# Due times of the rank work and the number of slot buffers in a one-core graph layer

## The chip, the cores and the metric

The kernel runs on one core of one Trainium2 chip. A core has five engines that run at the same time, each through its own list of instructions in a fixed order: PE (TensorE, the matrix unit), DVE (VectorE), ACT (ScalarE), POOL (GpSimd) and SP (SyncE, which here only issues transfers). Transfers between the chip's memory and the core's own memory are carried by DMA engines beside them. An instruction that needs another engine's result, or a transfer's data, waits on a semaphore, and everything behind it on its engine waits with it.

The metric is the device time of one execution in microseconds (us). The kernel before took 540.39 us, the median of three runs (539.81, 540.39 and 543.72).

## The reference

The layer is a graph convolution over 6250 nodes of 128 features and 100000 edges, which are sorted by destination:

```python
Xs = X[src]
m_data = Xs @ W_data.T + b_data
m_ctrl = Xs @ W_control.T + b_control
msg = jnp.where((edge_types == 0)[:, None], m_data, m_ctrl)
agg = jax.ops.segment_sum(msg, dst, num_segments=X.shape[0])
out = agg + (X @ W_self.T + b_self)
x = _layernorm(x + jax.nn.relu(out), axis=-1)
```

Each edge takes its source node's row, multiplied by one of two weight matrices by the edge's type; a destination sums its edges' rows, adds its own row times a third matrix, and the result is rectified, added to the input and normalized.

## The kernel before

The kernel gathers no row by address for most edges. It multiplies all nodes by both matrices once (`m3`: 98 blocks of 128 rows, each value kept as three bf16 parts of 128 columns, so 384 columns) and then gathers and sums with matrix products of 0/1 matrices.

**Ranges and groups.** The destinations are cut into 39 ranges of 160 nodes, numbered here from 0; a few nodes at the end are handled by a gather on POOL. The ranges form eleven groups of 1, 2 and then nine times 4 (`GROUPS`), numbered by an index from 0: index 4 holds ranges 11 to 14, index 5 (the sixth group) ranges 15 to 18, and index 10 ranges 35 to 38.

**Rank work** (`ranks`) prepares a group. For each edge of a range it finds in which of the 98 blocks the source lies and the edge's rank among the edges of that block. It loads the edges (`win`, L468), builds 0/1 matrices `hots` on DVE (L799, L803), counts on PE (L810), sends the counts to memory and back (`past`, L830 and L833), forms ranks on PE (`rk`, L846) that DVE reduces to slots (`slot`, L851), and scatters the source numbers on PE into `vt` (L890). DVE turns `vt` into `vs` (L905 to L911), and SP writes it to memory (`packed`, L917). PE multiplies once more into `vt` for the edges that found no slot (L993).

**A range's main work** (`sums`). SP copies the range's packed slots from memory to all 128 partitions (`rows<-packed`, L1043, 784 KB). DVE compares them in place with the partition number (L1053), which gives the 0/1 matrix of sources. In 25 steps PE multiplies it by `m3` (stage 1, L1075: four matmuls into one bank, `g` or `x`), ACT or DVE copies the bank to `gs` (L484, L485), and PE multiplies by the 0/1 matrix of destinations, `hot2` (built on DVE, L1061), into the sum `a` (stage 2, L1092 and L1095). After a range DVE adds the three parts (`s`, L624); after a group the rows are normalized, also with a product into `vt` (L615), and written.

**What sets the order.** Nothing in the code is in the order in which it runs. Each step is added to a plan with its engine, an estimated duration, a due number and what it reads and writes; `Plan.run` is a list scheduler that gives each engine the ready step with the lowest due number and writes all instructions in that order. The order on the chip is then fixed. Range number r has the due number `T0 + r * TW` with `T0` 36 and `TW` 13. The rank work of a group is due from `when` on:

```python
when = max(when + late + 22 * step + GAP, T0 + w0 * TW - LEAD)
```

Here `w0` is the group's first range and `LEAD` is 80, so from index 3 on rank work starts 80 units ahead of its range, and the groups are 52 units apart.

**Buffers.** A buffer ring gives a new tile the buffer of the tile that came so many before it, and the first writer of the new tile waits for all users of the old one. The packed slots have the ring `rows` with three buffers: the copy for range r can start when stage 1 of range r-3 is over. At the start of the kernel the same three buffers hold the first three of four pieces of the transposed input (`xts`), from which `m3` is made. `vt` and `rk` are one bank each, `hot2` has two buffers.

## Time and profile before

| | us |
|---|---|
| median of three runs | 540.39 |
| lowest and highest | 539.81 and 543.72 |
| the profiled execution | 542.22 |
| its span, first to last instruction | 540.4 |
| PE busy in the span | 502.1 |
| DVE busy | 441.1 |
| ACT busy | 429.0 |
| POOL busy | 201.5 |

A profile is one execution, recorded by the hardware. Its rows give the start and duration of each instruction, and by the semaphores what ended a wait. PEclk is the granted clock of PE as a share of full speed. Engine names with a q (SPq) are the engine's queue, which issues transfers and waits. A matmul's end is modelled, so that a PE that is shown as busy may still be waiting for a moment. The rows that carry the argument stand in the prediction.

### The profile page before, as it was taken

The page shows a single profiled execution, that of the slowest core. Times are in us where ns is not written, and L with a number is a line of the kernel's source. Part 1 is how long each engine was busy: PE and PEld are TensorE (multiplying, and loading weights), DVE is VectorE, ACT ScalarE, POOL GpSimd, SP SyncE. Part 2 cuts the span into 40 slices and gives each one's busy share as a digit, 9 for nine tenths or more (in the row PEclk, how much of TensorE's full clock was granted, in tenths as well). Part 3 has the DMA queues.
Part 4 walks back from the last instruction along what each step waited for, and adds up shares of the span by engine and source line. Part 5 has one row for each costly group of instructions (what it writes and reads, how often), then busy time and mean ns, then how long its engine had stood idle before and what let it go on. Part 6 is the DMA issues. An engine that isn't in the chain of part 4 may idle for free. (4 is left out here: it accounts for less than half of the span.)

```text
span 540.4 us, 30907 instructions
## 1 busy us (share of the span) xinstructions
PE 502.1 (93%) x13288; PEld 432.6 (80%) x13288; DVE 441.1 (82%) x1168; ACT 429.0 (79%) x1077; POOL 201.5 (37%) x284
## 2 busy tenths in 40 slices
PE   7799879799999988999999999999999999999991
PEld 4465557699889877888988887888898899888990
DVE  6388989889989997898989889979978678956642
ACT  4566767698889877888988878978898898878990
POOL 1000535700830684176067247707701720542000
PEclk9989899999999998999999999999999999999997
DMA  7466661540453055325413533351342352234200
GB/s 244 160 256 224 240 181 29 167 161 6 134 145 88 12 139 151 98 77 152 141 38 111 141 95 95 91 180 41 115 128 88 115 163 89 63 107 126 70 19 17
DMA packets 44932, 63.43 MB, mean 117 GB/s; under 512 B 19178, under 2 KB 35279, under 8 KB 44751
## 3 DMA queue, kind: packets, MB, share of 16 engines
q1 hardware_dynamic: 41745, 56.22, 33.5%
q0 software_dynamic: 1120, 2.23, 2.0%
q10 hardware_dynamic: 1922, 2.91, 1.7%
q8 instruction: 106, 1.74, 1.3%
q14 instruction: 39, 0.32, 0.2%
HBM read 45.61 MB, written 13.82 MB: 110 GB/s over the span
## 5 line engine op out<-in xcount | busy, mean ns | idle before, releaser
L1092 PE MATMUL a<-gs,hot 128*32 128x384 bf16 x3744 | 376.1, 328 | 0.4 <-issue 0.3
L484 ACT CAST gs<-g 128x384 bf16<-128x384 f32 x700 | 302.9, 492 | 64.3 <-PE g L1075 53.6
L1075 PE MATMUL g<-m,rows 128*32 128x384 bf16 x2958 | 327.1, 336 | 9.0 <-DVE rows L1053 5.7
L1075 PEld LDWEIGHTS <-rows 128*32 128x32 bf16 x3822 | 253.4, 134 | 27.7 <-DVE rows L1053 6.5
L1095 PE MATMUL a<-gs,hot 128*32 128x128 bf16 x2808 | 273.1, 220 | 2.1 <-issue 2.1
L1092 PEld LDWEIGHTS <-hot 128*32 128x32 bf16 x3900 | 206.4, 98 | 6.7 <-issue 3.1
L1095 PEld LDWEIGHTS <-hot 128*32 128x32 bf16 x2925 | 155.6, 97 | 14.1 <-issue 2.4
L1075 PE MATMUL x<-m,rows 128*32 128x384 bf16 x864 | 122.0, 335 | 0.0
L484 ACT CAST gs<-x 128x384 bf16<-128x384 f32 x199 | 98.3, 494 | 8.6 <-PE x L1075 5.7
L1061 DVE TENSOR_TENSOR hot<-iota_b,to_d 128x1920 bf16<-128x1920 bf16 (+2 forms) x85 | 93.1, 1105 | 0.1
L851 DVE TENSOR_REDUCE slot<-rk 124x8 f32<-124x400 f32 (+2 forms) x99 | 56.1, 567 | 22.3 <-PE g L1075 10.3
L674 POOL TENSOR_SCALAR xr<-xr,mv,rstd 128x128 f32<-128x128 f32 (+1 forms) x44 | 56.5, 1289 | 21.9 <-DVE rstd L651 18.4
L846 PE MATMUL rk<-hots,tri 128*32 128x400 bf16 (+1 forms) x388 | 51.3, 337 | 4.5 <-DVE slot L851 1.5
L1053 DVE TENSOR_SCALAR rows<-rows,pid 128x3136 bf16<-128x3136 bf16 (+1 forms) x46 | 41.6, 904 | 5.7 <-DMA rows<-packed 5.7
L937 POOL TENSOR_SCALAR pv<-slot 124x88 f32<-124x88 bf16 x9 | 9.5, 1058 | 79.6 <-DVE slot L868 74.2
L624 DVE TENSOR_REDUCE s<-a 128x128 f32<-128x384 f32 (+1 forms) x40 | 22.1, 551 | 15.7 <-ACT bs L484 9.9
L1016 POOL DMA_INDIRECT sr<-table,at x20 | 29.8, 1489 | 10.8 <-DVE at L1004 6.2
L491 POOL COPY to_d<-vs 32x100 bf16<-32x100 bf16 (+1 forms) x72 | 29.2, 406 | 5.9 <-DVE vs L911 2.7
L846 PEld LDWEIGHTS <-tri 128*32 128x32 bf16 x428 | 22.9, 96 | 9.9 <-issue 8.6
L803 DVE TENSOR_TENSOR hots<-hots,val 124x1200 bf16<-124x1200 bf16 (+3 forms) x42 | 28.0, 675 | 0.0
L799 DVE TENSOR_TENSOR hots<-iota_b,st 124x1200 bf16<-124x1200 bf16 (+3 forms) x42 | 27.6, 671 | 0.0
L767 POOL TENSOR_SCALAR pay<-u 124x88 f32<-124x88 f32 x9 | 8.9, 994 | 46.2 <-DVE u L752 45.1
(224 smaller groups left out, 667.9 us busy)
## 6 DMA issues: line engine op xcount, KB each, us to landing
rows<-packed SPq DMA_DIRECT2D x36, 784.0 KB
table<-m SPq DMA_DIRECT2D x12, 768.0 KB
xc<-in_xt SPq DMA_DIRECT2D x9, 320.0 KB
rows<-packed ACTq DMA_DIRECT2D x3, 784.0 KB
rows<-in_xt SPq DMA_DIRECT2D x8, 256.0 KB
xr<-in_x SPq DMA_DIRECT2D x8, 256.0 KB
out<-xr SPq DMA_DIRECT2D x8, 256.0 KB
gl<-sr SPq DMA_DIRECT2D x39, 48.0 KB
```

The lines of the kernel that those rows point to most:

```text
L484: [("ACT", act(cols), lambda: A.copy(o(), src())), ("DVE", dve(cols), lambda: V.tensor_copy(o(), src()))], None, None, due, r, w, lat)
L491: "POOL", 0.25 + cols * 0.0014, lambda: G.tensor_copy(o(), src()), due, r, w)
L674: fp = lambda k=k, m=m: G.tensor_scalar(h.t[:m, k, :], h.t[:m, k, :], mv.t[:m, k, 0:1], rstd.t[:m, k : k + 1], op0=ALU.subtract, op1=ALU.mult)
L803: vec(when + 2 + pace * k0, m * NC, lambda k0=k0, k1=k1, hs4=hs4, hp=hp: V.tensor_tensor(hp(), hp(), fl(val)[:, k0 * nw : k1 * nw, None, : ...
L846: T.matmul(acc.t[R * j : R * j + R, : (k1 - k0) * wide], tri.t[:, R * j : R * j + R], flat(k0, k1, P), start=True, stop=True, skip_group_c ...
L851: vec(due, (k1 - k0) * wide, lambda k0=k0, k1=k1, acc=acc: V.tensor_reduce(slot.t[:, k0:k1, :], acc.t[:EP, : (k1 - k0) * wide].rearrange(" ...
L1016: add("POOL", GC, lambda pr=pr, sr=sr: G.indirect_dma_start(out=sr.t[: room(pr)], out_offset=None, in_=table[:, :], in_offset=bass.Indirec ...
L1053: add("DVE", dve(half * NT, 0.305) + 0.05, lambda sp=sp, rs=rs: V.tensor_scalar(sp.t[:, rs], sp.t[:, rs], pid1.t, None, op0=ALU.is_equal), ...
L1061: lambda i=i, hot2=hot2, s4=s4, c0=c0, c1=c1: V.tensor_tensor(hot2.t[:, c0:c1].rearrange("p g (c d) -> p g c d", d=2), iota1_b.t.rearrange ...
L1075: T.matmul(gp.t[R * t : R * t + R, :D3], sp.t[:, :, 4 * g + t], m3.t[:, 4 * g + t, :], start=True, stop=True)
L1092: T.matmul(a.t[R * j : R * j + R, :D3], hot2.t[:, g, R * j : R * j + R], gs.t, start=g == 0, stop=False, skip_group_check=True)
L1095: T.matmul(a.t[R * c : R * c + R, D3:], hot2.t[:, g, P:], gs.t[:, c * D : (c + 1) * D], start=False, stop=last, skip_group_check=True)
```

## The change

The due number of a group's rank work is lowered by 4 for index 5, by 8 for index 6, and so on to 24 for index 10; from index 4 on the groups are so 48 apart, not 52. The ring of packed slots has two buffers. The third piece of the transposed input, which had its third buffer, gets a tile of its own.

```diff
     for j, n in enumerate(XB):
-        ring = ("rows", 3, R * NT) if j < 3 else ("hot2", 2, NS * WN)
-        xts.append(B(work, [D, 2 * n * P], BF16, *ring))
+        if j == 2:
+            xts.append(C([D, 2 * n * P], BF16, "x2"))
+        else:
+            ring = ("rows", 2, R * NT) if j < 2 else ("hot2", 2, NS * WN)
+            xts.append(B(work, [D, 2 * n * P], BF16, *ring))
...
-            sp = B(work, [P, R, NT], BF16, "rows", 3, R * NT)
+            sp = B(work, [P, R, NT], BF16, "rows", 2, R * NT)
...
-            when = max(when + late + 22 * step + GAP, T0 + w0 * TW - LEAD)
+            when = max(when + late + 22 * step + GAP, T0 + w0 * TW - LEAD - 4 * max(gi - 4, 0))
```

No instruction of the computation is added or taken away. The scheduler writes a new order, with line numbers three higher behind the first edit. Three places show what moves.

The first is SP's list where the packed slots of index 4 are written and the copies for ranges 11 and 12 follow. `past` and `hots` belong to index 5, `win` loads the edges of index 6. Before:

```order
L917 DMA packed<-vs 128x2x98
L462 TENSOR_LOAD first
L468 ISA
L468 DMA win<-in_edges 124x66
L830 DMA past<-csb 64x2x200
L462 TENSOR_LOAD first
L468 ISA
L468 DMA win<-in_edges 124x66
L1043 DMA rows<-packed 128x3136 x2
L833 DMA hots<-past 4x4400
```

Now, from `past` of the same group on:

```order
L833 DMA past<-csb 64x2x200
L462 TENSOR_LOAD first
L468 ISA
L468 DMA win<-in_edges 124x66
L836 DMA hots<-past 4x4400
L920 DMA packed<-vs 128x2x98
L1046 DMA rows<-packed 128x3136
```

The copy for range 11 stood behind two loads and `past`, and now follows the write of the slots directly; that write itself now stands behind `past` and `hots`, and the copy for range 12 comes later.

The second is DVE's list around the compare of range 11 (`rows<-rows,pid`). Before, `hot_6187` is the destination matrix of range 11, `hot_6280` that of range 12, and `s<-a` the end of range 10:

```order
L1061 TENSOR_TENSOR hot_6187<-iota_b,to_d 128x2080
L1061 TENSOR_TENSOR hot_6187<-iota_b,to_d 128x1920
L803 TENSOR_TENSOR hots<-hots,val 124x1200
L624 TENSOR_REDUCE s<-a 128x128
L1061 TENSOR_TENSOR hot_6280<-iota_b,to_d 128x2080
L1053 TENSOR_SCALAR rows<-rows,pid_129 128x3136
L633 SCALAR_TENSOR_TENSOR xr<-s,xr 128x128
```

Now, where `hot_6206` is the destination matrix of range 11:

```order
L854 TENSOR_REDUCE slot<-rk 124x8
L1064 TENSOR_TENSOR hot_6206<-iota_b,to_d 128x2080
L854 TENSOR_REDUCE slot<-rk 124x8
L1056 TENSOR_SCALAR rows<-rows,pid_129 128x3136
L854 TENSOR_REDUCE slot<-rk 124x8
L1064 TENSOR_TENSOR hot_6206<-iota_b,to_d 128x1920
L854 TENSOR_REDUCE slot<-rk 124x8
L627 TENSOR_REDUCE s<-a 128x128
```

The compare of range 11 stood behind the end of range 10 and the first half of range 12's matrix, and now stands ahead of both, between four slot reductions of index 5.

The third is SP's list later, where the slots of index 7 (ranges 23 to 26) are written. Before, the three copies are those of ranges 22, 23 and 24:

```order
L1043 DMA rows<-packed 128x3136
L597 DMA xr<-in_x 128x4x128
L604 DMA xr<-in_x 32x128 x4
L917 DMA packed<-vs 128x2x98
L1043 DMA rows<-packed 128x3136
L607 DMA xb<-in_xt 128x4x32
L830 DMA past<-csb 64x2x200
L1043 DMA rows<-packed 128x3136
L833 DMA hots<-past 4x4400
```

Now they are those of ranges 21, 22 and 23:

```order
L1046 DMA rows<-packed 128x3136
L920 DMA packed<-vs 128x2x98
L1046 DMA rows<-packed 128x3136
L833 DMA past<-csb 64x2x200
L836 DMA hots<-past 4x4400
L610 DMA xb<-in_xt 128x4x32
L1046 DMA rows<-packed 128x3136
```

The write of a group's slots now comes a range earlier against the copies, and each copy is issued one range nearer to its use.

## The prediction

> **What bounds the kernel now.** I read the page first, for the busiest engine.

> ```profile
> PE 502.1 (93%) x13288; PEld 432.6 (80%) x13288; DVE 441.1 (82%) x1168; ACT 429.0 (79%) x1077; POOL 201.5 (37%) x284
> ```

> PE is busy for 93% of the span, and the change takes no instruction from it. So it can win only where PE stands still or is slowed. The second view cuts the span at the last stage 2 matmul of every fourth range (windows: start and end, length, then busy time of each engine with counts, granted clock, DMA share and GB/s). These are the stretches of ranges 7 to 10, 11 to 14, 15 to 18, 19 to 22, and 35 to 38.

> ```profile
> 155.60:200.60 45.00, 44.95 (x1330) 41.67 (x1320) 42.77 (x104) 39.38 (x101) 17.86 (x30) 1.00 0.30 82
> 200.60:253.90 53.30, 48.66 (x1371) 42.15 (x1373) 45.88 (x108) 41.46 (x105) 28.41 (x35) 0.97 0.42 119
> 253.90:300.50 46.60, 45.95 (x1343) 41.15 (x1338) 42.33 (x101) 40.24 (x104) 23.80 (x31) 1.00 0.37 107
> 300.50:348.40 47.90, 46.96 (x1366) 40.41 (x1360) 43.69 (x106) 40.71 (x105) 26.61 (x32) 1.00 0.37 112
> 487.50:527.50 40.00, 39.30 (x1150) 36.59 (x1140) 22.46 (x52) 35.82 (x92) 3.92 (x5) 1.00 0.23 68
> ```

> Four ranges take 45 to 48 us with another group's rank work among them, 40.0 without. Since the work among them only moves, its price on PE moves with it. One stretch stands out: ranges 11 to 14 take 53.3 us, 6.7 more than the next four, at a mean clock of 0.97. Third, the timeline there, SP's queue, then DVE, then the matmul that PE waited to start:

> ```profile
> 189.37 0.40 SPq L917 DMA_DIRECT2D packed<-vs  x1
> 190.46 0.28 SPq L468 DMA_DIRECT2D win<-in_edges  x1
> 193.36 0.66 SPq L830 DMA_DIRECT2D past<-csb  x1
> 195.12 0.30 SPq L468 DMA_DIRECT2D win<-in_edges  x1
> 195.52 1.91 SPq L1043 DMA_DIRECT2D rows<-packed  x2
> ...
> 200.43 0.78 DVE L803 TENSOR_TENSOR hots<-hots,val 124x1200 bf16<-124x1200 bf16 x1
> 201.12 0.55 DVE L624 TENSOR_REDUCE s<-a 128x128 f32<-128x384 f32 x1
> 201.59 1.23 DVE L1061 TENSOR_TENSOR hot<-iota_b,to_d 128x2080 bf16<-128x2080 bf16 x1
> 202.74 1.03 DVE L1053 TENSOR_SCALAR rows<-rows,pid 128x3136 bf16<-128x3136 bf16 x1
> ...
> 203.83 0.71 PE L1075 MATMUL g<-m,rows 128*32 128x384 bf16 x12 [3.21 <-DVE rows L1053]
> ```

> The slots of range 11 are written at 189.37, but their copy is issued at 195.52, behind two loads and `past`; DVE then does other work first, compares at 202.74, and PE has stood still for 3.21 us. What follows the stop is in finer windows:

> ```profile
> 196.00:200.00 4.00, 4.00 (x129) 3.34 (x124) 3.92 (x8) 3.62 (x9) 3.87 (x4) 1.00 0.94 202
> 200.00:204.00 4.00, 0.79 (x23) 0.50 (x19) 4.00 (x7) 0.26 (x1) 3.90 (x3) 1.00 1.03 306
> 204.00:208.00 4.00, 3.66 (x62) 2.64 (x62) 3.32 (x6) 2.20 (x5) 3.53 (x4) 0.59 0.92 295
> 208.00:212.00 4.00, 4.00 (x123) 3.42 (x119) 2.90 (x8) 3.65 (x10) 0.70 (x1) 0.98 0.44 87
> ```

> For 4 us the granted clock is 0.59 and PE does 62 matmuls, not 123.

> **The change part by part.** *The stop at range 11.* In the new order the copy follows the write of the slots directly. It still waits for that write to land, and it can start, since range 9's stage 1 is over there. From issue to a waiting DVE a copy takes 4.88 us, then comes the compare, by the chain of waits (start, duration) at another range:

> ```profile
> 350.90 4.88 DMA rows<-packed
> 355.80 1.04 DVE rows L1053
> 356.84 0.49 DVE slot L851
> ...
> SPq L1043 <- DMA packed<-vs: 15.5, 8, 2.5
> SPq L833 <- DMA past<-csb: 9.7, 5, 2.9
> ```

> The write lands in 15.5 / 8 = 1.9 us. Issued at 189.4 + 0.4 + 1.9 = 191.7, the copy would be at DVE by 196.6 and compared by 197.6, 3.0 us before PE needs it at 200.6. The write stands behind `hots` now, which waits up to 2.9 us for `past`; then it is 200.5, just in time. On DVE the compare stands behind three slot reductions of about 0.5 us, the last of which needs a rank product late in range 10. So the 3.2 us go, with a rest between 0 and 2; I take 0.3, since it is the reductions that are left, and the other work that stood ahead is behind.

> *The clock.* 123 - 62 = 61 matmuls were missing in 4 us, at 4.00 / 123 = 0.0325 us each: 2.0 us. They go if the stop goes.

> *The rest of that stretch.* Of 6.7 us, 3.2 and 2.0 are named; 1.5 is left, waits behind the stop. I count half, 0.8, between 0 and 1.5.

> [...] Single stops in this trace: 3.32 us and 3.21 us were followed by half clock, 2.25 us was not (rows: the stop's end, and the window behind it).

> ```profile
> 26.53 0.70 PE L545 MATMUL g<-w_sb,rows 128*128 128x256 f32 x2 [3.32 <-DVE m L565]
> 78.89 0.55 PE L1075 MATMUL g<-m,rows 128*32 128x384 bf16 x8 [2.25 <-DVE rows L1053]
> ...
> 27.20:30.60 3.40, 3.40 (x10) 2.05 (x8) 2.78 (x8) 1.66 (x3) 0.00 (x0) 0.50 0.80 280
> 79.50:83.00 3.50, 3.48 (x96) 3.07 (x91) 3.50 (x6) 3.22 (x9) 0.17 (x1) 1.00 0.47 137
> ```

> [...]

> *Two buffers.* Every copy from range 4 on now waits for stage 1 of the range before the last, one range later than before. Issue to compared is 4.88 + 1.04 = 5.9 us; at range 11, where copies queued, it was 203.8 - 195.5 = 8.3. A range lasts 46.6 / 4 = 11.7 us, or 40.0 / 4 = 10.0 at the end. So 4 to 6 us are left before PE waits, 1.7 in the crowded case, and copies can no longer queue behind each other, since the next waits for a range's end. Nothing is paid while DVE is not that late. But DVE's list is in order: where it comes to the compare before the copy has landed, it stands.

> ```profile
> DVE rows L1053 <- DMA rows<-packed: 5.7, 5, 2.8
> SPq L1043 <- PE g L1075: 84.2, 23, 9.2
>   DVE slot L851: 1.3, 1
> ```

> DVE stood so for 5.7 us in five cases, and one, 2.8 us at 352.96, made PE wait 1.3 us for `slot` (last row, the rank products at 356). In the new order this wait may go, -1.3, or the five may double, +5.7 if all of it reached PE. I take +1.0, near the one that did. Behind a copy that waits on SP (84.2 us in 23 cases already) stand writes of slots, `past` and `hots` of later groups, and loads of inputs; the third place of the order shows them a range ahead of their users, so I price them at nothing, and if that cover is gone they cost what the same kind costs in the line for `hots`, up to 2.9 us once.

> *Rank work ahead.* It moves, PE's price with it, from ranges 32 and 33 forward. It meets DVE, 42 of 46.6 us busy in a middle stretch and 22.46 of 40.0 in the last. Its DVE share is squeezed from 52 to 48 units, so 42.33 us at most grow to 42.33 x 52 / 48 = 45.9, still under 46.6: nothing. The earlier first piece in `rows` and its own tile change no wait at the start that I can see: nothing.

> *The sum.* -3.2 + 0.3 - 2.0 - 0.8 + 1.0 = -4.7 us. The profiled execution, 542.22 us with 1.8 us around its span of 540.4, would be 537.5. The median, 540.39, is 1.8 below that execution, so I forecast 540.39 - 4.7 = 535.7 us.

> **The rivals.** *More goes.* PE also waits for the bank `vt`:

> ```profile
> PE vt L615 <- DVE vs L908: 2.1, 3, 0.8
> ```

> In the new order the product L615 comes after `vt`'s other users from index 5 on, half a range or more behind the scatter. If these 2.1 us and the 1.3 us at 356 go too, it is 535.7 - 2.1 - 1.3 = 532.3. Against it: another product now follows the scatter closely and can wait for the same DVE work.

> *The stop only moves*, to range 12, whose copy now waits for range 10 and stands behind more loads of edges, each of which can wait for DVE. Then 5.2 us are not won: 540.9 us.

> *The clock has another cause*: 535.7 + 2.0 = 537.7.

> *Slower: the buffers.* DVE, nearly full between 155 and 350 us, reaches the compare more than 4 us after the landing, in most ranges. From that point each range costs the excess; at 0.4 us on 36 ranges, 14.4: 550.1. The row for it is the stop at 200.6, where DVE was the one that was late; against it, the copy landed late there too. [...]

> **How the numbers follow.** The forecast holds 0.47, more goes 0.22, the stop moves 0.18, the clock 0.05, the buffers 0.08. Faster or slower means here by over 1%, 5.4 us, about what a measurement of this kernel can tell from no change; the bound is 535.0. The forecast's own range, 534 to 538 by the rest of 0 to 2 and the 1.5, has 0.10 of its chance below it. Faster: 0.22 + 0.10 = 0.32; slower: 0.08; the same: 0.60. The range goes from 532, where all that is named goes, to 541.4, the moved stop with 0.5 for the runs' spread; the buffers lie outside.

> **What would show it.** Right: in the changed profile PE starts range 11 with under 1 us of wait for the compare, PEclk there is 1.00, and ranges 11 to 14 take about 48 us. Waits of DVE for the copies between 4 and 12 us in total, most of them without a PE wait. Wrong: a PE wait for `rows` above 2 us anywhere behind range 4, above all one that repeats; a stretch of four ranges over 50 us; or the clock low without a stop.

## The result and the profile after

The changed kernel takes 542.42 us, the median of 22 runs, against 540.37 us for 22 runs of the kernel before on the same chips: a ratio of 1.0055, with a 95% interval of 1.0038 to 1.0072. It is slower by half a per cent, where 535.7 us was forecast, and above the range of 532 to 541.4. The profiled execution took 544.98 us, its span 543.2. Medians here and below are over all runs of a kernel; ratios and their intervals leave out the runs over 1.5% above its fastest.

The page, engines and granted clock:

```profile
PE 504.8 (93%) x13288; PEld 438.8 (81%) x13288; DVE 439.8 (81%) x1167; ACT 429.9 (79%) x1078; POOL 198.4 (37%) x284
...
PEclk9989899999999999999999999999999999999997
```

The same line before:

```profile
PEclk9989899999999998999999999999999999999997
```

The low digit in the middle, half clock behind the stop at range 11, is gone. The same stretches as before, ranges 7 to 10, 11 to 14, 15 to 18, 19 to 22 and 35 to 38 (window: length, then busy time of each engine with counts, granted clock, DMA share, GB/s):

```profile
154.67:201.27 46.60, 46.37 (x1353) 40.91 (x1347) 42.68 (x105) 39.82 (x103) 19.91 (x34) 1.00 0.36 105
201.27:249.33 48.06, 47.06 (x1365) 42.24 (x1359) 43.94 (x106) 41.62 (x107) 27.97 (x33) 1.00 0.39 114
249.33:298.28 48.95, 46.98 (x1352) 41.36 (x1346) 43.38 (x105) 40.52 (x105) 21.87 (x34) 1.00 0.40 114
298.28:349.84 51.56, 47.70 (x1364) 43.83 (x1358) 43.81 (x110) 41.71 (x107) 26.30 (x32) 1.00 0.34 99
491.44:530.51 39.07, 39.07 (x1149) 38.57 (x1139) 23.20 (x53) 35.75 (x92) 3.89 (x5) 1.00 0.26 83
```

Ranges 11 to 14 fell from 53.3 to 48.06 us. But ranges 15 to 18 rose from 46.6 to 48.95, and 19 to 22 from 47.9 to 51.56. The changed kernel is 4.6 us ahead at the end of range 14 (249.33 against 253.9) and behind by 3 at the end of range 38 (530.51 against 527.5).

At range 11 the timeline has what was forecast (SP's queue, then DVE):

```profile
189.56 0.40 SPq L920 DMA_DIRECT2D packed<-vs  x1
192.19 0.35 SPq L1046 DMA_DIRECT2D rows<-packed  x1
...
199.30 0.56 DVE L854 TENSOR_REDUCE slot<-rk 124x8 f32<-124x400 f32 x1
199.78 1.09 DVE L1056 TENSOR_SCALAR rows<-rows,pid 128x3136 bf16<-128x3136 bf16 x1
200.95 0.57 DVE L854 TENSOR_REDUCE slot<-rk 124x8 f32<-124x400 f32 x1
```

The copy is issued 2.2 us after SP has issued the slots' write, and the compare ends at 200.87, before PE needs it at 201.27. The windows there show no stop and full clock, where PE stood for 3.21 us and the clock was 0.59 in 204 to 208:

```profile
200.00:204.00 4.00, 4.00 (x114) 3.49 (x109) 3.92 (x9) 3.49 (x11) 3.53 (x4) 1.00 0.70 196
204.00:208.00 4.00, 4.00 (x115) 3.58 (x109) 4.00 (x8) 3.60 (x10) 2.38 (x2) 1.00 0.72 209
```

The new waits, by the view of waits (total, count, longest) and by PE's timeline:

```profile
DVE hr L977 <- POOL pos L971: 6.4, 6, 2.6
PE vt L996 <- DVE hr L977: 3.1, 3, 1.5
```

```profile
324.36 0.63 PE L996 MATMUL vt<-f,hr 124*64 124x3 bf16 x24 [1.52 <-DVE hr L977]
355.98 0.23 PE L1098 MATMUL a<-gs,hot 128*32 128x128 bf16 x2 [1.79 <-issue]
```

The first kind is rank work. `pos` (L971) is a small POOL operation that stands behind the eight POOL copies of a group into `to_d` (L491); DVE's `hr` needs it, and PE's listed products (L996) need `hr`. In the second PE waited for nothing that the profile shows; the profile writes "issue" there. The experiments are about both kinds.

### The profile page after: what moved, and what is told of

The parts are those of the page before. It is cut to its first block, busy times and chain, and to the rows that moved or that the text cites. A ratio compares the mean times of both kernels' runs of the same rounds, so it can differ in the third digit from the quotient of the medians.

```text
span 543.2 us, 30923 instructions
## 1 busy us (share of the span) xinstructions
PE 504.8 (93%) x13288; PEld 438.8 (81%) x13288; DVE 439.8 (81%) x1167; ACT 429.9 (79%) x1078; POOL 198.4 (37%) x284
## 3 DMA queue, kind: packets, MB, share of 16 engines
q8 instruction: 106, 1.74, 1.3%
## 4 chain that ended last, share of the span: by engine, by line
PE 75%; DVE 7%; POOL 7%; DMA 4%; issue 2%; ACT 2%; ACTq 0%; DVEq 0%; POOLq 0%
PE g L1078 26%; PE a L1095 23%; PE x L1078 8%; PE a L1098 4%; POOL to_d L491 4%; PE rk L849 4%; PE vt L893 2%; DMA past<-csb 2%; PE g L548 2%; PE a L584 2%; DMA hots<-past 1%; PE vt L996 1%; ACT gs L484 1%; DVE hr L977 1%; DVE hot L1064 1%
## 5 line engine op out<-in xcount | busy, mean ns | idle before, releaser
L1098 PE MATMUL a<-gs,hot 128*32 128x128 bf16 x2808 | 289.9, 219 | 2.9 <-issue 2.8
L1078 PEld LDWEIGHTS <-rows 128*32 128x32 bf16 x3822 | 265.8, 134 | 24.6 <-issue 9.9
L1095 PEld LDWEIGHTS <-hot 128*32 128x32 bf16 x3900 | 216.8, 97 | 8.0 <-issue 5.0
L1098 PEld LDWEIGHTS <-hot 128*32 128x32 bf16 x2925 | 171.2, 97 | 11.6 <-issue 3.4
L484 ACT CAST gs<-x 128x384 bf16<-128x384 f32 x204 | 101.1, 496 | 15.9 <-PE x L1078 8.7
L1064 DVE TENSOR_TENSOR hot<-iota_b,to_d 128x1920 bf16<-128x1920 bf16 (+2 forms) x85 | 94.4, 1113 | 0.0
L677 POOL TENSOR_SCALAR xr<-xr,mv,rstd 128x128 f32<-128x128 f32 (+1 forms) x44 | 55.7, 1273 | 46.8 <-DVE rstd L654 39.3
L940 POOL TENSOR_SCALAR pv<-slot 124x88 f32<-124x88 bf16 x9 | 10.6, 1180 | 76.8 <-DVE slot L871 76.7
L491 POOL COPY to_d<-vs 32x100 bf16<-32x100 bf16 (+1 forms) x72 | 35.6, 494 | 8.5 <-DVE vs L914 3.1
L1019 POOL DMA_INDIRECT sr<-table,at x20 | 22.1, 1104 | 12.9 <-DVE at L1007 7.2
L770 POOL TENSOR_SCALAR pay<-u 124x88 f32<-124x88 f32 x9 | 7.2, 805 | 43.1 <-DVE u L755 42.0
```

The lines of the kernel that those rows point to most:

```text
L484: [("ACT", act(cols), lambda: A.copy(o(), src())), ("DVE", dve(cols), lambda: V.tensor_copy(o(), src()))], None, None, due, r, w, lat)
L491: "POOL", 0.25 + cols * 0.0014, lambda: G.tensor_copy(o(), src()), due, r, w)
L677: fp = lambda k=k, m=m: G.tensor_scalar(h.t[:m, k, :], h.t[:m, k, :], mv.t[:m, k, 0:1], rstd.t[:m, k : k + 1], op0=ALU.subtract, op1=ALU.mult)
L1064: lambda i=i, hot2=hot2, s4=s4, c0=c0, c1=c1: V.tensor_tensor(hot2.t[:, c0:c1].rearrange("p g (c d) -> p g c d", d=2), iota1_b.t.rearrange ...
L1078: T.matmul(gp.t[R * t : R * t + R, :D3], sp.t[:, :, 4 * g + t], m3.t[:, 4 * g + t, :], start=True, stop=True)
L1095: T.matmul(a.t[R * j : R * j + R, :D3], hot2.t[:, g, R * j : R * j + R], gs.t, start=g == 0, stop=False, skip_group_check=True)
```

## The experiments

Each kernel was timed beside the kernel before on the same chip. There were five chips for the experiments, so kernels are best compared by their ratios to before and not by their medians. A stretch runs from the end of one range's last stage 2 matmul to that of another, in the one profiled execution of a kernel.

### The halves, a constant shift, and POOL's copies later

The first two kernels each have one half of the change. The shift alone, against the kernel before:

```diff
-            when = max(when + late + 22 * step + GAP, T0 + w0 * TW - LEAD)
+            when = max(when + late + 22 * step + GAP, T0 + w0 * TW - LEAD - 4 * max(gi - 4, 0))
```

> The due times of the changed kernel with three buffers and the first tile layout of before. In the changed kernel ranges 15 to 30 take 197.4 us against 187.9 before. Theory A (the rank work that is moved ahead packs its last links, eight copies on POOL, pos, DVE's hr and PE's listed products, into lists that run in order, and PE and DVE stand for them): the stop at range 11 is gone and the loss behind range 14 is there all the same: ranges 15 to 30 at 194 to 199 us, 541 to 544 us in all. Theory B (the loss is from two buffers): ranges 15 to 30 at 187 to 190 us, 534 to 537 us. Theory C (no one cause, a planner's list that comes out otherwise): anywhere from 536 to 545, with waits at places that neither kernel has.

Two buffers alone, with a tile of its own, `x2`, for the third piece of the input (the expectation calls it the first); against the changed kernel:

```diff
-            when = max(..., T0 + w0 * TW - LEAD - 4 * max(gi - 4, 0))
+            when = max(..., T0 + w0 * TW - LEAD)
```

> Two buffers and the first piece's own tile, with the due times of before. The copy of range 11 stands behind one load here, not behind two loads and past. A: ranges 15 to 30 take 187 to 190 us as before; at range 11 the stop shrinks to 0 to 2 us; 536 to 540 us. B: ranges 15 to 30 take 194 us or more, 543 to 548 us. C: 536 to 545 with new places of waiting.

A constant shift, and POOL's copies later, each against the changed kernel:

```diff
-            when = max(..., T0 + w0 * TW - LEAD - 4 * max(gi - 4, 0))
+            when = max(..., T0 + w0 * TW - LEAD - 4 * (gi > 4))
```

> The changed kernel with every group from the sixth on four us ahead, and no growth from group to group. The order ahead of range 11 is that of the changed kernel, so the stop there is gone by every theory. A: the loss behind range 14 shrinks with the growth: 2.35 us of it (ranges 15 to 18) may stay, the rest goes: ranges 15 to 30 at 188 to 192 us, 536 to 539 us. B: the loss stays whole, 541 to 544 us. C: in between, without order.

```diff
-                     .to_broadcast([R, pn, nx, 2]), pn * nx * 2, d2 + 2, [vs],
+                     .to_broadcast([R, pn, nx, 2]), pn * nx * 2, d2 + 6 * (gi >= 5) + 2 * (gi < 5), [vs],
```

> The changed kernel with the eight copies into to_d four units later in POOL's due times from the sixth group on, so that pos stands ahead of most of them. The changed kernel's PE waits 3.1 us for hr in three places, and DVE 6.4 us for pos. A: these waits fall under 1 and 3 us, and 2 to 4 us of the loss are won: 538 to 540.5 us. B and C: the waits for hr may fall, the time stays at 541.5 to 543.5 us.

| kernel | median, us | ratio to before | 95% interval | ranges 11-14 | 15-30 | 31-38 |
|---|---|---|---|---|---|---|
| before | 537.94 | 1 | | 53.3 | 187.9 | 85.7 |
| shift alone | 545.37 | 1.0128 | 1.008 to 1.0176 | 49.5 | 195.2 | 82.8 |
| two buffers alone | 530.96 | 0.9869 | 0.9819 to 0.9918 | 47.7 | 187.5 | 86.3 |
| changed (its own runs) | 542.42 | 1.0055 | 1.0038 to 1.0072 | 48.1 | 197.4 | 83.8 |
| constant shift | 538.04 | 0.9992 | 0.9958 to 1.0026 | 46.6 | 193.8 | 85.1 |
| copies later | 532.89 | 0.9894 | 0.9847 to 0.9942 | 46.8 | 191.8 | 81.3 |

Two buffers alone win 1.3%; the shift alone loses 1.3%. For both, ranges 15 to 30 came as theory A had them (195.2 and 187.5 us), and the times did not: 545.37 us is above its 541 to 544, and 530.96 is below what any of the three theories had. The constant shift has a time within A's range, but its ranges 15 to 30 take 193.8 us, where A had 188 to 192. The windows of ranges 15 to 30, two buffers alone and then the changed kernel:

```profile
246.24:433.77 187.53, 183.54 (x5378) 165.17 (x5373) 161.22 (x384) 160.18 (x413) 86.27 (x117) 1.00 0.36 110
```

```profile
249.33:446.71 197.38, 188.52 (x5448) 170.65 (x5442) 167.80 (x395) 162.44 (x415) 84.29 (x118) 1.00 0.35 104
```

So the loss goes with the shift, and theory B falls. Two buffers alone also shrink the stop at range 11, since the copy no longer stands behind `past` and the second load of edges; the rest is 0.55 us (SP's queue, DVE, and PE's wait):

```profile
186.94 0.40 SPq L920 DMA_DIRECT2D packed<-vs  x1
188.03 0.28 SPq L468 DMA_DIRECT2D win<-in_edges  x1
188.95 0.36 SPq L1046 DMA_DIRECT2D rows<-packed  x1
```

```profile
198.06 1.01 DVE L1056 TENSOR_SCALAR rows<-rows,pid 128x3136 bf16<-128x3136 bf16 x1
...
199.13 0.71 PE L1078 MATMUL g<-m,rows 128*32 128x384 bf16 x12 [0.55 <-DVE rows L1056]
```

The copies later look like the proof of theory A: `pos` now runs behind three copies, not eight. The same place in group index 5, changed and with copies later:

```profile
223.40 4.98 POOL L491 COPY to_d<-vs 32x100 bf16<-32x100 bf16 x8 [1.41 <-DVE vs L914]
228.46 0.27 POOL L971 TENSOR_TENSOR pos<-iota_f,pos_all 124x48 bf16<-124x48 f32 x1
```

```profile
220.33 1.12 POOL L491 COPY to_d<-vs 32x100 bf16<-32x100 bf16 x3 [1.41 <-DVE vs L914]
221.54 0.37 POOL L971 TENSOR_TENSOR pos<-iota_f,pos_all 124x48 bf16<-124x48 f32 x1
221.97 3.78 POOL L491 COPY to_d<-vs 32x100 bf16<-32x100 bf16 x5
```

But PE's waits for `hr` fell only from 3.1 to 1.5 us in all, and the time by 1.6%, some 8.7 us (0.9894 / 1.0055), where A expected 2 to 4. Something else moved too.

### Other ways to the same chain

> The changed kernel with pos on DVE from the sixth group on, so that hr no longer stands behind the eight copies on POOL; all else as changed. In the changed kernel the way from prefix to listed products on PE took 5.45 to 9.03 us in groups 5 to 10, against 3.58 to 3.99 before. A (the chain through POOL is late, and DVE and PE stand for it in order): that way falls under 4.5 us, PE's wait for hr (3.1 us) and DVE's wait for pos (6.4 us) are gone, ranges 15 to 30 take 188 to 193 us against 197.4, and the time is 533 to 538 us. C (any other order of the planner would have cured it): the waits go, the time stays within 1 us of the changed kernel's.

```diff
-        vp(gi >= 2, d3, nw * EL * 2, lambda e: e.tensor_tensor(
+        vp(2 <= gi < 5, d3, nw * EL * 2, lambda e: e.tensor_tensor(
```

> The changed kernel with hr and the listed products due four units later from the sixth group on: POOL's chain is as late as in the changed kernel, but DVE and PE have other work in front of what hangs on it. A: PE's and DVE's waits shrink by at least half, ranges 15 to 30 take 190 to 194 us, 535 to 539 us. If what costs is not these waits in order but that the chain itself ends late (to_d, the gathers, and what hangs on them): no change, 541 to 544 us.

```diff
+        d5 = d3 + 4 * (gi >= 5)
-        vec(d3, nw * EL * LIST, lambda: V.tensor_tensor(
+        vec(d5, nw * EL * LIST, lambda: V.tensor_tensor(
...
-        add("PE", 0.0235 * nw * EL, listed, d3, [hl, f4], [sp_ps])
+        add("PE", 0.0235 * nw * EL, listed, d5, [hl, f4], [sp_ps])
```

> The changed kernel with two us a group for four (2 to 12 us ahead). If the size of the shift sets the loss, it lies between that of no shift (531.0 with two buffers) and that of four a group (about 542): 535 to 538 us, ranges 15 to 30 at 190 to 194 us. If what sets it is where a group's prefix and listed products fall among the close products, the loss follows that place and not the shift: where prefix to listed is 4 us or less in most groups it is 531 to 534 us, where it is over 5.5 us, 538 to 543 us.

```diff
-            when = max(..., T0 + w0 * TW - LEAD - 4 * max(gi - 4, 0))
+            when = max(..., T0 + w0 * TW - LEAD - 2 * max(gi - 4, 0))
```

> The faster half alone (two buffers, the due times of before) with pos on DVE in every group. With pos in front of nothing on POOL, prefix to listed falls to 2 to 3.5 us. A: little is left to win, since PE waits for hr nowhere in that half: 529 to 532 us. If DVE is the worse place (it is busy 82% of the span): 532 to 535 us.

```diff
-            when = max(..., T0 + w0 * TW - LEAD - 4 * max(gi - 4, 0))
+            when = max(..., T0 + w0 * TW - LEAD)
...
-        vp(gi >= 2, d3, nw * EL * 2, lambda e: e.tensor_tensor(
+        vp(False, d3, nw * EL * 2, lambda e: e.tensor_tensor(
```

The way from prefix to listed products, by the starts of both on PE, in groups of index 5 to 10:

| kernel | prefix to listed, us | ratio | 95% interval | ranges 15-30 |
|---|---|---|---|---|
| before | 3.6 to 4.0 | 1 | | 187.9 |
| two buffers alone | 2.9 to 4.3 | 0.9869 | 0.9819 to 0.9918 | 187.5 |
| changed | 5.5 to 9.0 | 1.0055 | 1.0038 to 1.0072 | 197.4 |
| constant shift | 5.8 to 6.7 | 0.9992 | 0.9958 to 1.0026 | 193.8 |
| copies later | 3.8 to 5.3 | 0.9894 | 0.9847 to 0.9942 | 191.8 |
| `pos` on DVE | 2.3 to 5.2, once 8.1 | 1.0057 | 1.0027 to 1.0087 | 199.5 |
| listed due later | 5.5 to 9.0 | 1.0064 | 1.003 to 1.0098 | 197.8 |
| two us a group | 5.6 to 7.3 | 1.0169 | 1.0117 to 1.0221 | 196.0 |
| two buffers, `pos` on DVE | 2.2 to 3.9 | 1.0009 | 0.9972 to 1.0046 | 191.2 |

Listed due later tells nothing of the theory: the lists of all five engines came out the same as the changed kernel's, presumably since these steps become ready later than their due numbers. It is the changed kernel a second time, and agrees with it (1.0064 and 1.0055).

Three expectations fail. Half the shift came out above the whole (1.0169 against 1.0055), and above both of its forecasts. `pos` on DVE on top of two buffers shortens the way, and the ratio rises from 0.9869 to 1.0009. And in the changed kernel `pos` on DVE shortens the way in every group, in one only from 9.0 to 8.1 us, and wins nothing, as theory C had it. PE stood elsewhere instead: at one place the wait went to `f` (L989), which the listed products also need and which POOL had not done in time:

```profile
320.39 0.60 PE L996 MATMUL vt<-f,hr 124*64 124x3 bf16 x24 [2.45 <-POOL f L989]
```

The windows behind this stop and behind one at 353.54 that is put to issue (1.86 us) show a granted clock of 0.52 and 0.60, where that of the changed kernel was full from 100 to 530 us:

```profile
355.40:358.80 3.40, 3.40 (x55) 2.81 (x59) 0.81 (x1) 1.88 (x4) 0.00 (x0) 0.52 0.02 5
320.40:323.80 3.40, 3.40 (x77) 3.27 (x80) 1.53 (x5) 0.96 (x2) 2.97 (x7) 0.60 0.00 0
```

At 0.52 and 0.60 of the clock these 6.8 us lost, by estimate, 3.4 x 0.48 + 3.4 x 0.40 = 3.0 us. Even without them ranges 15 to 30 would take 196.5 us. So none of these runs bears theory A out. They do not refute it either: each is one order at one place in PE's code, and the next section shows that this place alone moves an order by over 1%. Nor does the half shift show that its size does not matter, for the same reason: its waits put to issue, 12.15 us, are twice those of the changed kernel.

### What PE waits for when the row says issue

The waits of PE that are put to issue, summed behind 100 us from the traces, differ from kernel to kernel: 2.48 us before, 6.06 changed, 8.87 shift alone, 4.02 two buffers alone, 3.65 copies later, 7.51 with `pos` on DVE, 9.53 with that on two buffers, 12.15 with two us a group. The page's list of DMA queues has one of its own for code:

```profile
q8 instruction: 106, 1.74, 1.3%
```

That is 106 packets of 16 KB (1.74 MB in all), one for about 250 of PE's 26,576 matmuls and weight loads. They follow PE's count: by a line fitted through the starts of these packets in the traces of before and changed, without the first five, one starts for every 255.7 and 255.3 matmuls and weight loads. Around the wait of 1.79 us at 354.19 of the changed kernel, the windows:

```profile
349.00:352.60 3.60, 3.51 (x115) 2.96 (x111) 3.04 (x6) 2.60 (x7) 0.00 (x0) 1.00 0.86 276
352.60:354.20 1.60, 1.59 (x49) 1.15 (x37) 1.60 (x4) 1.26 (x4) 0.00 (x0) 1.00 0.92 287
354.20:356.00 1.80, 0.02 (x4) 0.02 (x6) 0.67 (x1) 0.37 (x1) 0.00 (x0) 1.00 0.06 13
```

A copy of a range's slots and another load fill the DMA engines to 0.86 and 0.92 until 354. The packet of code, the last one before PE goes on, starts at 353.56, 1.2 us behind the end of the copy's last packet (352.38) and while the other load still runs; PE stops at 354.19 and goes on at 355.98, 2.4 us behind the packet's start. Most of these stops look so. In 19 traces (all but the one with divided copies, below) the starts of such packets, counted against the end of each copy within reach (about 650 copies, of 3.1 to 3.5 us on the mean by kernel, from the first packet to the last), and the stops of over 0.6 us behind 100 us:

```
us against a copy's end     packets of code that start, all traces, mean per half us
-6.0 to -3.5                 79
-3.0 to -1.0                  9
-0.5 to +1.0                162
stops of PE put to issue, over 0.6 us:   69
  that end 2.15 to 2.70 us behind the start of a packet of code:   61
  whose packet starts -0.3 to +1.6 us from a copy's last packet:   58
```

The rates are starts per half us, summed over all these copies. While a copy moves, hardly any packet of code starts; they pile up at its end. The stops follow late packets closely, so theory D, in the expectations below, is that PE stands where it needs the code sooner. The longest of the stops is 2.87 us (the shift alone with 60 more instructions, below).

Which packet meets which copy should depend on where in PE's list one packet ends and the next begins. Four kernels shift these borders and nothing else: two of the five idle warming products at the start become 32 or 64 tiny ones, 60 or 124 more instructions ahead of all others. The order of every other instruction is word for word the same.

```diff
-        add("PE", 0.63, lambda: T.matmul(
+        add("PE", 0.63, lambda i=i: T.matmul(
...
-            skip_group_check=True), 0.01 * i, [idle], [warm])
+            skip_group_check=True) if i < 3 else [T.matmul(warm.t[:1, :1], idle.t[:, :1], idle.t[:, :1], start=True, stop=True, skip_group_check=True) for _ in range(16)], 0.01 * i, [idle], [warm])
```

> The changed kernel with the last two of the five idle warming products at its start made into 32 tiny ones (1x1): 60 more instructions on PE's list before anything else, the order of all other instructions word for word the same. PE's code arrives in packets of 16 KB, 106 in the run, about one for each 256 of its instructions. Theory D (PE runs out of code where the packet that it needs next is held back by a copy of rows, and which packet meets which copy sets the time): the waits put down to issue (6.06 us behind 100 us in the changed kernel, 1.79 at 354.19) change place, the one at 354 goes or shrinks, and the time moves by more than 0.3% (1.6 us), to 538 to 541 or 544 to 547 us. Theory A or C (waits for POOL, or the planner's order): nothing of the order has changed, so the time stays within 0.3% of the changed kernel, 541 to 544 us.

> The same with 64 tiny products, 124 more instructions, about half a packet. D: the waits put down to issue stand at other places than in the changed kernel and in the one with 60 more, and the three times spread over more than 3 us. A or C: all three within 1.6 us.

> The kernel before with 60 more tiny instructions on PE at its start, the order of the rest the same. Its waits put down to issue are 2.48 us behind 100 us, the least of all the orders seen so far but for none under it. D: they grow to 4 to 9 us with the other phase, and the time to 541 to 547 us; the kernel before was lucky in its phase, by up to what the change seemed to lose. A or C: 539 to 541.5 us.

> The kernel before with 124 more. D: another time again, with waits put down to issue between 2 and 9 us and the time following them at about one us for one us. A or C: 539 to 541.5 us.

The same was then done with two buffers alone, with the copies later, and with the shift alone.

> Two buffers with the due times of before, and 60 more tiny instructions on PE at the start, the order of the rest the same. The kernel with two buffers alone was at 0.987 of before, with 1.22 us of waits for issue in ranges 15 to 30; the kernel before went up by 1.0% with 60 more. If the buffers' gain is their own (the stop of range 11 and the half clock behind it gone, 5 us): ranges 11 to 14 stay under 50 us, and the time is 0.990 to 1.000 of before, 5 us under before with the same 60 more. If it was luck of the phase alone: 1.005 to 1.015, as before with 60 more.

> The same with 124 more. Own gain: 0.990 to 1.000 of before (before with 124 more was 1.009). Luck alone: 1.004 to 1.014.

> The changed kernel with the eight copies on POOL later, and 124 more instructions. The changed kernel went from 1.0055 to 1.019 of before with 124 more, the one with the copies later was at 0.989. If the later copies win by themselves what the moved rank work lost (ranges 15 to 30 at 191.8 us against 197.4): 0.995 to 1.005. If it was luck of the phase: 1.015 to 1.02.

> The due times of the changed kernel with three buffers, and 60 more tiny instructions. This half alone was at 1.013 of before. If the loss is the moved rank work's own: ranges 15 to 30 again at 193 to 198 us, and 1.005 to 1.020. If it was the phase: 0.995 to 1.003.

Ratios to the kernel before, with their intervals:

| order | no more | 60 more | 124 more |
|---|---|---|---|
| before | 1 | 1.0101 (1.0045 to 1.0157) | 1.0089 (1.0044 to 1.0134) |
| two buffers alone | 0.9869 (0.9819 to 0.9918) | 0.9942 (0.9921 to 0.9962) | 0.9934 (0.9907 to 0.996) |
| changed | 1.0055 (1.0038 to 1.0072) | 1.0079 (1.0044 to 1.0115) | 1.0189 (1.0132 to 1.0247) |
| copies later | 0.9894 (0.9847 to 0.9942) | | 1.0085 (1.0062 to 1.0109) |
| shift alone | 1.0128 (1.008 to 1.0176) | 1.0104 (1.0049 to 1.0159) | |

For ranges 3 to 38 of the one profiled execution, their length and then PE's waits put to issue behind 100 us:

| order | no more | 60 more | 124 more |
|---|---|---|---|
| before | 418.2, 2.48 | 427.0, 8.52 | 422.4, 7.00 |
| two buffers alone | 411.8, 4.02 | 413.4, 3.99 | 416.2, 5.38 |
| changed | 421.0, 6.06 | 423.0, 8.48 | 429.1, 12.51 |
| copies later | 412.3, 3.65 | | 424.1, 12.81 |
| shift alone | 422.1, 8.87 | 422.1, 9.07 | |

One order of work comes out up to 1.3% apart by the borders of its code alone (changed; copies later 1.9%), and within each order more waits put to issue go with a longer time of the same execution, but for the 0.03 us between the first two of two buffers. The changed kernel twice at the same borders came out 0.1% apart. Not all that D expected came: with 60 more the changed kernel moved by 0.24%, under D's bound of 0.3%, and the stop at 354 shrank to 0.33 us in the second execution at the same borders, so that one stop's going proves nothing. But the spread by order and border is there, where A and C expected none.

So the difference of 0.55% between before and changed is smaller than what the borders do to either: at equal borders the changed kernel takes 1.0055, 0.998 (1.0079 / 1.0101) and 1.010 (1.0189 / 1.0089) of before. What stands above it is seen at equal borders too; each such quotient is uncertain by 0.5 to 0.7%. Two buffers alone take 0.987, 0.984 and 0.985 of before (0.9942 / 1.0101, 0.9934 / 1.0089). The shift on top of two buffers costs 1.9, 1.4 and 2.6% (1.0055 / 0.9869 and so on). The copies later give back 1.6 and 1.0%; with 124 more they are at 1.0085, between their two forecasts. The shift with three buffers costs 1.3% and, with 60 more, nothing that stands out (1.0104 / 1.0101); its ranges 15 to 30 take 195.2 and 193.4 us, those of before 187.9 and 192.1.

### Copies in quarters, and rank work later

The first tests whether the length of a transfer is what holds the code back, on two buffers alone:

```diff
-                add(*Q[:2], lambda i=i, sp=sp, j=j, Q=Q: Q[2].dma_start(
-                    sp.t[P // RP * j : P // RP * (j + 1)].rearrange("p r c -> p (r c)"),
+                add(*Q[:2], lambda i=i, sp=sp, j=j, Q=Q: [Q[2].dma_start(
+                    sp.t[P // 4 * h : P // 4 * (h + 1)].rearrange("p r c -> p (r c)"),
...
-                    .rearrange("r c -> (r c)")[None, :].to_broadcast([P // RP, R * NT])),
+                    .rearrange("r c -> (r c)")[None, :].to_broadcast([P // 4, R * NT])) for h in range(4)],
```

> Two buffers with the due times of before, and each copy of a range's slots issued as four transfers of 196 KB one behind the other, in the place of the one of 784 KB; nothing else moves. In the fourteen traces so far hardly any packet of PE's code starts while a copy moves, and many start in the first 1.5 us behind its end. D1 (a packet of code waits for the transfer in front of it, and can go between two): packets of code start between the quarters, none is held for over 1 us, the waits for issue fall from 4.02 us to under 2 us, and the time by 1 to 3 us from that of two buffers alone, to 0.982 to 0.986 of before. D2 (it waits for all that the queue holds): as many packets are held for 3 us, and the time is that of two buffers alone or some us more, since SP issues four for one: 0.987 to 0.995.

Its ratio to before is 1.0001 (0.9965 to 1.0037), 1.3% above the whole copies and above what D1 and D2 had. Its twelve runs lie far apart, from 533.38 to 543.08 us, and the profiled one, at 542.43 us, is among the longest, so the sizes read from it may be larger than usual. The waits, first with quarters, then with whole copies:

```profile
DVE rows L1056 <- DMA rows<-packed: 15.2, 16, 2.1
...
PE rk L849 <- DVE slot L854: 4.5, 6, 0.9
```

```profile
DVE rows L1056 <- DMA rows<-packed: 4.7, 5, 1.7
...
PE rk L849 <- DVE slot L854: 0.4, 1, 0.4
```

Four transfers take 5.92 us from the first issue to the last packet, where one took 4.09 (medians of 28 copies). DVE stands for them 15.2 us, `slot` comes late, and PE pays 4.1 us more for it. Of 94 packets of code 26 start within a copy, over 0.3 us from its ends, of 96 with whole copies 9, so code does get in between; but the waits put to issue fell only from 4.02 to 3.35 us. D1 is right that code gets in and wrong on the gain, and whether shorter transfers would pay without the longer copy is open.

The second moves the rank work the other way, four us later from index 5 on, on two buffers:

```diff
-            when = max(..., T0 + w0 * TW - LEAD)
+            when = max(..., T0 + w0 * TW - LEAD + 4 * (gi > 4))
```

> Two buffers, and the rank work of every group from the sixth on four us later than before, where the change has it earlier. If rank work that comes earlier is what loses (1.9% over three phases between two buffers alone and the changed kernel), later may win: ranges 15 to 30 at 184 to 188 us, 0.980 to 0.990 of before. If the due times of before are about the best, or the waits only move to the compare of a group's first range: 0.990 to 1.005. The phase alone has moved two buffers by up to 0.7%.

It took 538.33 us, 0.9998 (0.9966 to 1.0031): later loses 1.3% as well, at the one border that was tried. Ranges 15 to 30 take 191.8 us, and PE stands at other places, the longest at the close product into `vt`:

```profile
320.68 0.53 PE L618 MATMUL vt<-bs,fold 96*32 96x128 f32 x8 [3.29 <-DVE vs L914]
```

So of the five sets of due times that were tried with two buffers, those of before came out best; but three of the other four were run at one border alone. The best version is two buffers alone: 530.96 us, 0.9869 of before, and under before at all three borders.

## Why the prediction was wrong

*The stop at range 11, -3.2 + 0.3, the clock, -2.0, and the rest of the stretch, -0.8.* Right in this profile. Summed, -5.7 us; ranges 11 to 14 fell by 5.2 (53.3 to 48.06) with full clock and no stop. The 2.0 for the clock is luck in part: in the kernel before with 124 more, PE waits 3.20 us at the same compare (until 200.51) and the granted clock behind it is 1.00 (201 to 205), so this loss need not come with the stop. The cause was also wider than the prediction had it: each half alone takes the stop at the compare away but for about half a us (0.55 with two buffers, 0.44 with the shift).

*Two buffers, +1.0.* Too dear. With two buffers alone DVE waits 4.7 us for copies in five cases, where it was 5.7 in five, and ranges 15 to 30 take 187.5 us, where they took 187.9. In the changed kernel DVE stood for no copy at all, by the last number of its row (busy, mean ns, idle before):

```profile
L1056 DVE TENSOR_SCALAR rows<-rows,pid 128x3136 bf16<-128x3136 bf16 (+1 forms) x46 | 41.6, 906 | 0.0
```

The rival that the buffers make it slower falls. The two waits of the rival that more goes, 2.1 us for `vs` at the close product and 1.3 for `slot`, are gone from the changed kernel's rows, and as its counter-argument had it, the prefix product now waits for `vs`, 1.0 us in two cases. The stop did not move to range 12.

*SP's queue, nothing.* Right as far as the runs show: in the changed kernel PE has no wait of over 0.15 us for a transfer behind range 4.

*Rank work ahead: "It moves, PE's price with it", and DVE's share stays under PE's, "nothing".* This is the step that failed. At the same borders of the code the shift costs 1.4 to 2.6% on top of two buffers; with three buffers, where it also takes the stop at range 11 away, it costs 1.3% at one border and nothing that stands out at another. By stretches of the profiles, means over the three borders, changed less two buffers alone: ranges 7 to 10 +1.3 us (46.9 less 45.6), 11 to 14 +1.8 (49.5 less 47.8), 15 to 30 +9.5 (197.7 less 188.2), 31 to 38 -2.4 (84.0 less 86.4), in all some +10 us. The prediction had work that only moves: a loss in some stretches, an equal gain in others. Most of the 9.5 us in the middle has no such counterpart. Of these, by sums over PE's waits in the same traces, 2.9 us are waits put to issue (4.6 against 1.6), 1.9 are waits for other engines (`hr` and `gs` above all), and 4.6 are time in which PE is shown as busy. At most 1.9 us of the last are work that came from ranges 31 to 38, where PE's busy time fell by as much; of the 84 rank products that are missing there, 64 are found in ranges 15 to 30. The other 2.7 us or more stand in no row.

The step compared busy times with the length of a stretch, and had no term for the order of the work. Rank work is a chain over four engines with lists in fixed order: between prefix and listed products lie eight POOL copies, `pos`, `hr` and `f`. In the new order prefix follows the scatter directly, the close product comes later, and the way from prefix to listed grew from 3.6 to 4.0 us to 5.5 to 9.0. That this way sets the price is not shown: `pos` on DVE shortened it and won nothing, at the one border that was tried. That the later copies win back 1.0 to 1.6% is shown, and not by which of their effects, since the scheduler moves other work with them. Why the shifted order has more waits put to issue is open too. So the step that failed is known, its price on two buffers is shown at three borders, and how the price comes about is known in part only.

*What was not in the prediction.* The borders of the code move an order by up to 1.9%. A sum of -4.7 us, 0.9%, can drown in that, and the prediction's range held nothing for it. Two buffers alone, the half of the change that the sum really described, came out 7.0 us under before at these borders (537.94 to 530.96, by medians of the same chip), and at 0.984 to 0.987 at equal borders.

*The signs.* Of the signs for right all came but one, since DVE waited for no copy of note. Of those for wrong one came, a stretch of four ranges over 50 us (51.56). It stood behind the stretch that the argument was about.

## What to carry to other kernels

Do not price moved work by an engine's free time alone: look also at the chain that it forms, link by link on each engine's list. Then try the parts of a change apart, since here one half won 1.3% by itself and the other cost 1.4 to 2.6% on top of it. Before an order is judged by a per cent, run it with a few dozen tiny instructions more at its start: where the time moves as much as the change did, the difference can't be put down to the order. Set waits that no row explains beside the queue that brings code and beside the long transfers; what to do about them is open, since shorter transfers won nothing here.

## What the runs showed of the hardware

POOL's copies into `to_d` took 406, 494 and 572 ns on the mean in three kernels. The row of all 72, before, changed, and with copies later:

```profile
L491 POOL COPY to_d<-vs 32x100 bf16<-32x100 bf16 (+1 forms) x72 | 29.2, 406 | 5.9 <-DVE vs L911 2.7 <-ACT gs L484 0.3
```

```profile
L491 POOL COPY to_d<-vs 32x100 bf16<-32x100 bf16 (+1 forms) x72 | 35.6, 494 | 8.5 <-DVE vs L914 3.1 <-DVE hots L802 2.5
```

```profile
L491 POOL COPY to_d<-vs 32x100 bf16<-32x100 bf16 (+1 forms) x72 | 41.2, 572 | 8.4 <-DVE vs L914 3.5 <-DMA t_msg<-table,t_idx 1.7
```

Of the 432 copies of the first six traces, 52 lay for over half their time beside DVE's reduction `s` and took 0.26 us each, 71 beside the comparison `hot2` and took 0.98. The comparison reads two tiles (`iota_b` and `to_d`), the reduction one (`a`); what makes the difference is not shown.

Single stops of 1.86 and 2.45 us were followed by half clock (0.52 and 0.60 in the two windows above), while behind those of 1.99 and 2.04 us (shift alone at 200.30, two us a group at 449.91) the granted clock was 1.00, as behind 2.25 us in the kernel before. At the compare of range 11, 3.21 us before was followed by half clock (0.59 on the mean of 204 to 208), and 3.20 us with 124 more was not (1.00 in 201 to 205). In these traces no length of one stop decides it.
